# A planned order of two transformers: value matmuls in one set, one PSUM pool, new lag and lead, earlier layer set-up, and a clock in the planner

## Chip, cores and metric

The kernel runs on one core of a Trainium2 chip. The metric is the device time in microseconds of one execution; the median of three runs is compared. Profiles come from one more execution, recorded by the hardware profiler.

## What is computed

The reference is a chain of eight residual stages on `x` of shape 2 x 512 x 128. Stages 4 and 6 are transformers of six layers (`_L2_xcond_ref` and `_L3_xcond_ref`, the same code with other weights), and the change touches only these and the planner that orders their instructions. Each layer has self-attention over 512 tokens, cross-attention to a context of 154 tokens, and a feed-forward part, 16 heads of 8 channels:

```python
for i in range(NL):                       # NL = 6
    xn = _adaln(x, noise_emb, n1_w[i], n1_b[i])
    q, k, v = jnp.split(xn @ qkv_w[i].T, 3, axis=-1)
    a = _attn(_rope(q), _rope(k), v, src_mask).reshape(B, L, D) @ so_w[i].T
    x = x + a
    xn = _adaln(x, noise_emb, n2_w[i], n2_b[i])
    q = _rope((xn @ cq_w[i].T).reshape(B, L, H, HD))
    k = _rope((context @ ck_w[i].T).reshape(B, LC, H, HD))
    v = (context @ cv_w[i].T).reshape(B, LC, H, HD)
    a = _attn(q, k, v, ctx_mask).reshape(B, L, D) @ co_w[i].T
    x = x + a
    xn = _adaln(x, noise_emb, n3_w[i], n3_b[i])
    h = jax.nn.gelu(xn @ f1_w[i].T + f1_b[i], approximate=False)
    x = x + (h @ f2_w[i].T + f2_b[i])
```

(The reshapes of the self-attention are cut.) `_attn` is a softmax over scaled scores, times the values; all is f32.

## The kernel before

A layer is four blocks in the order self-attention of batch 0, of batch 1, cross-attention of batch 0, of batch 1 (`blocks`). A block has four groups of four heads (`Group`). A group passes through two streams.

*Maxima.* For each 128 queries and each head a matmul scores all keys with queries on the partitions (`maximum`: 29 rows of the array, output 512 columns, in a self block; two tiles of 154 in a cross block), and VectorE takes the negated maximum along the keys into `mx`. After the last one, `close` transposes `mx` into `mxT` and four DMAs on SP's queue write it into a spare row of `qT`. A self group has 16 such steps, a cross group 8.

*Exponents.* For each chunk of keys (four chunks of 128 in a self block, two of 77 in a cross block) and each head a matmul scores with keys on the partitions (`exp`: 32 rows, the row with the maxima included, so that the score comes out with its maximum taken off), and ScalarE writes exp of it to a tile `p`. After a chunk's four heads, four value matmuls (128 rows of the array by 32 columns, one for each head, side by side) add the chunk to `av`. `finish` transposes `av` on VectorE and divides by the sum of the exponents. An exponent step of a group is again one head: 16 in a self group, 8 in a cross group.

The driver (the last `with nc.stretch()`) takes one step of each stream in turn; exponents start `LAG` = 24 steps after maxima, and each step adds `STEP` = 0.9 to the turn. When a block's exponents end, `after` projects, adds the residual and, in a cross block, does the feed-forward part, which the next layer's self block of that batch needs; `before` normalises and projects queries, keys and values ahead of a block's first maximum, and its results reach `qT` and `kT` by DMA. `before`, `after`, `close` and `finish` are marked as due `LEAD` = 22 turns earlier. A `Layer` object loads the layer's weights into one of two buffers `lw`, and makes the scale and shift `gb` with twelve small matmul instructions; it is made when the layer's first block is.

Nothing of this sets the order directly. Inside `stretch` all instructions are collected, and `Plan.order` simulates the five queues with estimated durations: it repeatedly takes, over all engines, the ready instruction with the earliest start plus `URGENCY` = 40 ns for each turn. Instructions under `together` are one set and stay adjacent. The plan knows tile buffers (an instruction can't start before all its tiles have a free buffer, and a score matmul also claims the SBUF tile that its evacuation will write), the four by four cells of the TensorE array, and 100 ns for a change of the array's shape. The order is made once for both transformers and issued as planned; `flush` (L344) issues everything, so nearly all rows of the profile carry that line.

PSUM has two pools in these stages: `ms` with seven banks for all scores and projections, and `av` with one. Tiles `p` come from a pool of 16.

In the profile every f32 matmul shows as two instructions: 96 self groups x 4 chunks x 4 heads are 1536 value matmuls, and their row says x3072.

## Time and profile before

| what | value |
|---|---|
| median of three runs (lowest, highest) | 3848.19 us (3847.7, 3848.45) |
| profiled execution | 3844.95 us, span 3843.2 us |
| mean granted TensorE clock | 0.896 |
| first maxima matmul of the first transformer, of the second | 803.2 us, 2322.3 us |
| last exponent (ScalarE, tile p) of the second transformer | 3656.5 us |

Row `p<-ms` of the page's costliest groups is ScalarE's exponents (1211.7 us busy, 606 ns each), `mx<-ms` VectorE's maxima (1297.1 us, 610 ns each), `ms<-kT,qT` and `ms<-kcT,qT` are the maxima's scores, `ms<-qT,kT` and `ms<-qT,kcT` the exponents' scores, and `av<-p,vp` and `av<-p,vcp` the value matmuls. Names ending in c belong to cross blocks. In a timeline, bracketed times are an engine's idle time before a piece and what ended it.

### The profile page before, as it was taken

How to read it: one execution, taken by the hardware profiler on the slowest of the kernel's cores; microseconds unless marked ns; L12 is line 12 of the kernel's file. 1: busy time of each engine (PE TensorE's matmuls, PEld its weight loads, DVE VectorE, ACT ScalarE, POOL GpSimd, SP SyncE). 2: the span in 40 equal slices, each digit the busy share in tenths (PEclk: the TensorE clock that was granted, in tenths of full speed). 3: DMA queues.
4: the chain of work that ended last, by engine and by line, in shares of the span. 5: the costliest groups of instructions: out<-in, count | busy, mean ns of one | idle time of the engine just before them, and what ended most of it. 6: DMA issues, size and time to landing. Idle time of an engine off the chain costs nothing.

```text
span 3843.2 us, 57110 instructions
## 1 busy us (share of the span) xinstructions
PE 3455.9 (90%) x21539; PEld 1931.9 (50%) x21539; DVE 2459.2 (64%) x5712; ACT 1758.4 (46%) x3268; POOL 563.6 (15%) x516
## 2 busy tenths in 40 slices
PE   5598999889999999999999739999999999999937
PEld 3333555455555545555555315555555555555526
DVE  5514555377586766867767477667686776768632
ACT  1122545335455454555545314545455454555550
POOL 2213767310100100010010010010100101010000
PEclk8698999979799988989989768989899998989968
DMA  1000000100000100000000100000000100000002
GB/s 38 1 28 22 1 1 1 38 12 5 10 22 8 28 7 23 10 10 23 8 11 6 42 0 12 8 22 10 11 22 8 28 7 23 10 10 7 8 20 77
DMA packets 179496, 61.01 MB, mean 16 GB/s; under 512 B 169475, under 2 KB 173367, under 8 KB 177559
## 3 DMA queue, kind: packets, MB, share of 16 engines
q1 hardware_dynamic: 177400, 54.72, 6.3%
q8 instruction: 171, 2.80, 0.3%
q10 hardware_dynamic: 1519, 1.74, 0.1%
q14 instruction: 102, 0.84, 0.1%
q0 software_dynamic: 304, 0.92, 0.1%
HBM read 36.37 MB, written 0.52 MB: 10 GB/s over the span
## 4 chain that ended last, share of the span: by engine, by line
PE 67%; DVE 6%; ACT 3%; issue 1%; DMA 1%; POOL 1%; SPq 0%; DVEq 0%; ACTq 0%; POOLq 0%
PE ms L344 50%; PE av L344 14%; PE ms L124 2%; ACT p L344 1%; PE big L124 1%; DVE gate L124 1%; DVE mx L344 1%; DVE avT L344 1%; DVE nrm L344 1%; DMA qT<-rows 1%; ACT L124 0%; DVE ln_st L344 0%; POOL ln_rs L344 0%; DVE aT L344 0%; SPq L344 0%
## 5 line engine op out<-in xcount | busy, mean ns | idle before, releaser
L344 ACT ACTIVATE p<-ms 128x512 f32<-128x512 f32 (+1 forms) x2304 | 1211.7, 606 | 857.5 <-PE ms L344 843.9
L344 DVE TENSOR_REDUCE mx<-ms 128x1 f32<-128x512 f32 (+2 forms) x2316 | 1297.1, 610 | 266.3 <-PE ms L344 256.1
L344 PE MATMUL ms<-qT,kT 32*128 32x512 f32 (+1 forms) x3096 | 933.9, 640 | 3.9 <-ACT p L344 2.4
L344 PE MATMUL ms<-kT,qT 29*128 29x512 f32 x3072 | 916.1, 689 | 13.6 <-DMA qT<-rows 9.0
L344 PEld LDWEIGHTS ms<-qT,kT 32*128 32x128 f32 (+1 forms) x3096 | 382.8, 186 | 231.9 <-ACT p L344 79.5
L344 PEld LDWEIGHTS ms<-kT,qT 29*128 29x128 f32 x3072 | 399.7, 197 | 196.3 <-DVE mx L344 78.9
L344 PE MATMUL ms<-kcT,qT 29*128 29x154 f32 x3072 | 397.3, 347 | 2.8 <-ACT p L344 1.5
L344 PEld LDWEIGHTS ms<-kcT,qT 29*128 29x128 f32 x3072 | 352.8, 209 | 62.7 <-ACT p L344 36.8
L344 POOL TENSOR_TENSOR ln_rs<-ln_ve,mhalf 128x4 f32<-128x4 f32 x96 | 97.7, 1021 | 1899.5 <-DVE ln_ve L344 1899.4
L344 PE MATMUL ms<-qT,kcT 32*77 32x512 f32 x1536 | 352.4, 710 | 9.3 <-DVE mx L344 9.1
L344 PE MATMUL av<-p,vp 128*32 128x512 f32 x3072 | 351.6, 595 | 0.0
L344 DVE STREAM_TRANSPOSE avT<-av 128x512 f32<-128x512 f32 x192 | 137.3, 715 | 237.5 <-PE av L344 235.7
L344 POOL TENSOR_SCALAR p<-p,s 128x666 f32<-128x666 f32 x128 | 249.3, 1960 | 106.7 <-DVE s L344 106.6
L344 PE MATMUL av<-p,vcp 77*32 77x512 f32 x1536 | 229.2, 671 | 2.8 <-DVE avT L344 2.6
L344 PEld LDWEIGHTS av<-p,vp 128*32 128x32 f32 x3072 | 89.3, 109 | 214.5 <-issue 212.2
L344 PEld LDWEIGHTS ms<-qT,kcT 32*77 32x77 f32 x1536 | 117.2, 163 | 124.2 <-issue 67.0
L344 ACT ACTIVATE nrm_t<-ms,gb 128x512 f32<-128x512 f32 x72 | 56.3, 782 | 255.9 <-PE ms L344 238.1
L344 POOL TENSOR_TENSOR turned<-rope_a,rope_s 128x256 f32<-128x256 f32 x144 | 101.3, 728 | 453.6 <-DVE rope_s L344 453.6
L344 DVE TENSOR_TENSOR Y<-Y,ms 128x512 f32<-128x512 f32 x72 | 49.5, 687 | 171.8 <-PE ms L344 171.8
L344 ACT ACTIVATE p<-big,m 128x666 f32<-128x666 f32 x128 | 103.7, 814 | 116.1 <-DVE m L344 115.9
L344 DVE TENSOR_REDUCE m<-big 128x1 f32<-128x666 f32 x128 | 104.1, 846 | 81.7 <-PE big L344 81.7
L344 PE MATMUL ms<-ident,nrm 128*128 128x128 f32 x344 | 76.5, 351 | 74.6 <-DVE nrm L344 71.6
(336 smaller groups left out, 3563.4 us busy)
## 6 DMA issues: line engine op xcount, KB each, us to landing
lw<-in_layers SPq DMA_DIRECT2D x12, 1413.0 KB
ew<-in_w SPq DMA_DIRECT2D x24, 512.0 KB
qT<-rows SPq DMA_DIRECT2D x192, 64.0 KB
qT<-mxT SPq DMA_DIRECT2D x768, 2.0 KB
kT<-rows SPq DMA_DIRECT2D x96, 64.0 KB
wkv<-in_wkv SPq DMA_DIRECT2D x1, 1024.0 KB
f2b<-in_f2b SPq DMA_DIRECT2D x12, 64.0 KB
rv<-in_rows POOLq DMA_DIRECT2D x1, 640.0 KB, 7.3
```

Of the source, the lines that this page charges most:

```text
L124: return getattr(getattr(self._plan.real, self._name), method)(*a, **k)
L344: getattr(getattr(self.real, op.lane), op.method)(*op.a, **op.k)
```

## The change

- The value matmuls of all chunks of a group are issued in one `together` set after the group's last exponent, at the current turn instead of 2.5 later; `av` is taken from the pool `ms` at that moment.
- The pools are eight banks of `ms` and none of `av`.
- 22 tiles `p` instead of 16.
- `LEAD` 30 instead of 22, `LAG` 28 instead of 24.
- `Layer(l + 1)` is made ahead of the first cross block of layer l.
- The planner keeps the use of the array in windows of 3413.3 ns; after a window below 0.42, and in the first, it takes a matmul as twice as long.

```diff
-LEAD, LAG, STEP = 22.0, 24, 0.9
+LEAD, LAG, STEP = 30.0, 28, 0.9
...
+    WINDOW, ENOUGH = 3413.3, 0.42
...
+        use, slow = [0.0], [True]
+
+        def pace(s):
+            w = int(s / self.WINDOW)
+            while len(use) <= w:
+                slow.append(use[-1] < self.ENOUGH)
+                use.append(0.0)
+            return 2.0 if slow[w] else 1.0
...
                     s = max(s, last)
+                    pe = op.takes * pace(s)
+                    use[int(s / self.WINDOW)] += op.takes * len(op.cells) / 16.0 / self.WINDOW
                     for c in op.cells:
-                        cells[c] = s + op.takes + (op.fill if s > last + 10.0 else 0.0)
+                        cells[c] = s + pe + (op.fill if s > last + 10.0 else 0.0)
...
-                done = s + op.takes + op.lands
+                done = s + (pe if op.cells else op.takes) + op.lands
...
-        wide, deep = (2, 3, 1), (0, 7, 1)
+        wide, deep = (2, 3, 1), (0, 8, 0)
...
-                self.tc.tile_pool(name="tfp", bufs=16) as many:
+                self.tc.tile_pool(name="tfp", bufs=22) as many:
...
-                    me.av = self.av.tile([P, 512], F32, name="av")
+                    me.ps = []
...
                         if jj[-1] == 3:
-                            nc.at(turn[0] + 2.5)
+                            me.ps.append(p)
+                        if c == nch - 1 and jj[-1] == 3:
+                            me.av = self.bank()
+                            nc.at(turn[0])
                             with nc.together():
-                                for j in range(4):
-                                    at = (4 * me.g + j) * (HD + 1)
-                                    nc.tensor.matmul(me.av[32 * j:32 * j + 32], lhsT=me.block.vp[:rows, c, at:at + 32], rhs=p[j][:rows],
-                                                     start=c == 0, stop=c == nch - 1)
+                                for c1, p1 in enumerate(me.ps):
+                                    for j in range(4):
+                                        at = (4 * me.g + j) * (HD + 1)
+                                        nc.tensor.matmul(me.av[32 * j:32 * j + 32], lhsT=me.block.vp[:rows, c1, at:at + 32], rhs=p1[j][:rows],
+                                                         start=c1 == 0, stop=c1 == nch - 1)
...
             def blocks():
-                layers = {}
-                for l in range(NL):
-                    for own in (True, False):
-                        for b in range(B):
-                            if l not in layers:
-                                layers[l] = Layer(l)
-                            yield Block(layers[l], b, own)
+                layers = [Layer(0)]
+                for x in range(2 * NL):
+                    l, cross = divmod(x, 2)
+                    for b in range(B):
+                        if b == 0 and cross and l + 1 < NL:
+                            layers.append(Layer(l + 1))
+                        yield Block(layers[l], b, not cross)
```

## The prediction

> **What bounds the kernel now.** I read the core's span and clock first, then the page's busy shares and the chain that ended last, then a table of windows over one transformer layer, and last the timelines of TensorE (PE) and ScalarE (ACT) around one group.

> ```profile
> span 3843.2 us, 57110 instructions
> PE 3455.9 (90%) x21539; PEld 1931.9 (50%) x21539; DVE 2459.2 (64%) x5712; ACT 1758.4 (46%) x3268; POOL 563.6 (15%) x516
> ...
> PE ms L344 50%; PE av L344 14%; PE ms L124 2%; ACT p L344 1%; PE big L124 1%; DVE gate L124 1%; DVE mx L344 1%; DVE avT L344 1%; DVE nrm L344 1%; DMA qT<-rows 1%; ACT L124 0%; DVE ln_st L344 0%; POOL ln_rs L344 0%; DVE aT L344 0%; SPq L344 0%
> ```

> PE looks like the bound: 90% busy, and scores (ms) with value products (av) are 64% of the chain. But the score matmuls use 32 rows of the array each, and several can run at once, so busy time overstates the need. The windows show stages (columns: us, then busy time and instruction count of PE, PEld, DVE, ACT, POOL, the granted clock, DMA share, GB/s).

> ```profile
> 803.00:2142.00 1339.00, 1306.58 (x8790) 734.95 (x8794) 945.23 (x2110) 682.83 (x1276) 99.10 (x126) 0.90 0.07 13
> 2322.00:3631.00 1309.00, 1278.03 (x8818) 715.89 (x8820) 947.22 (x2115) 684.39 (x1280) 99.09 (x126) 0.93 0.07 13
> ...
> 1529.00:1645.00 116.00, 115.12 (x851) 63.98 (x846) 93.86 (x193) 67.24 (x130) 7.17 (x10) 1.00 0.06 9
> 1645.00:1684.00 39.00, 37.48 (x288) 23.05 (x284) 24.48 (x66) 19.40 (x37) 2.43 (x3) 0.78 0.06 9
> 1684.00:1720.00 36.00, 35.12 (x263) 18.13 (x256) 19.63 (x59) 22.48 (x43) 6.97 (x9) 1.00 0.04 6
> 1720.00:1757.00 37.00, 34.67 (x137) 20.03 (x136) 24.43 (x50) 9.47 (x14) 2.28 (x2) 0.73 0.19 52
> ```

> The two transformers hold 2648 of 3843 us. A layer is 228 us: 116 of self-attention groups at full clock with VectorE (DVE) 81% busy, then self to cross (39 us, clock 0.78), cross groups (36), and cross to the next layer (37, clock 0.73, ACT busy 9.5). So I see two losses: inside the self groups, and at the two boundaries of a layer.

> Inside a group, PE's timeline and ACT's:

> ```profile
> 1583.15 0.90 PE L344 MATMUL ms<-qT,kT 32*128 32x512 f32 x2
> 1583.58 2.86 PE L344 MATMUL ms<-kT,qT 29*128 29x512 f32 x15
> 1586.37 3.64 PE L344 MATMUL av<-p,vp 128*32 128x512 f32 x32
> 1589.94 1.99 PE L344 MATMUL ms<-qT,kT 32*128 32x512 f32 x14
> ...
> 1591.16 1.08 ACT L344 ACTIVATE p<-ms 128x512 f32<-128x512 f32 x2 [6.30 <-PE ms L344]
> ```

> PE issues a group's last exponent score (qT,kT) at 1583.15, fills the free banks with maxima scores (kT,qT), does all value products in one run (32 instructions, two per matmul, are all four chunks), and only then issues exponent scores again, 6.8 us later. ACT starves 6.3 us. In PE's timeline 86 of the 96 self groups have this one run of 32, with a median of 6.48 us between the last exponent score before it and the first after. The reason is in the code: pool `many` has 16 tiles p, a group needs 4 chunks x 4 heads = 16, so the next group's first exponent has no tile to write until value products have read one. It is a shortage of p, not of PE.

> [...] 8 value instructions took 1.07 us and 16 took 1.92, so a run costs 2 x 1.07 - 1.92 = 0.22 us beyond its work. [...]

> **The change part by part.** Base: the profiled execution, 3845.0 us with 1.8 outside its span; the median of the runs is 3.2 above it.

> *Value products together, 22 tiles p.* Most self groups already have one run, so joining them is not the main point. Runs still split: 10 self groups (16+16) and 41 cross groups (8+8), 51 in all. Each joined pair saves the 0.22 us[...]: 11 to 23 us, taken 15. The six extra tiles matter more: six exponents (0.50 to 0.57 us each on ACT, 5.01 us for 10 and 4.58 for 8 in ACT's timeline), 3.3 us of ACT work, can be scored before the value products and run beside them. Seven consecutive self periods of a layer are 18.5, 16.8, 17.8, 14.9, 15.2, 14.4 and 13.4 us (every 32nd exponent instruction), mean 15.9, so 84 periods in 12 layers. DVE, 81% busy, becomes the limit at 0.81 x 15.9 = 12.9 us, so the most to gain is 3.0 us a period, 252 us. The least is 0: the six exponents run early, the tiles run out again, and ACT idles just as long before the value run. The planner decides, since a value run waits for the array to drain (a score matmul is two passes of 0.43 us) plus 100 ns in its model, while a score can start at once; turns count 40 ns each, so some maxima still go ahead of the value run. I take 1.2 us a period, two fifths of the most: 100 us.

> *One pool of eight banks.* Before, one bank is a group's `av` from close to finish; after, it is held only from the value run to DVE's transpose (3.64 + 0.72 us and a queue of maxima), and is a score bank otherwise. Gain: one more score in flight. Price: the run can find all eight banks full and wait for one evacuation, 0.6 us (8.46 us for 14 maxima); behind it on PE's queue stand the next scores. Over 84 periods between -25 and +50; I take 0, since the gain and the price concern the same bank.

> *Lead 30.* Projections, norms and feed-forward are due 8 turns (320 ns) sooner. At lead 22 the edge is 880 ns, about the price of draining two passes (0.86 + 0.10), so such a matmul may lose to one more score; at 1200 ns it wins. A boundary's path has about six such PE steps. With 22 boundaries inside the transformers, 0 to 4 us each, I take 1.5: 33 us.

> *Lag 28.* Exponents start four steps later. At each transformer's start maxima run alone and at its end exponents alone, four steps of about 0.55 us at each: 4 x 0.55 x 4 = 9 us more. In the steady state the exponents wait for no maximum now (PEld waits 4.2 us in all for mxT), so nothing is gained there.

> *Layer half a layer ahead.* The weights do not come sooner: for layers 2 to 5 their DMA already waits for the buffer that the layer two before leaves (issued at 1518.4 for a first use at 1691.2). What moves is both DMAs' place in SP's queue, which that wait fixes anyway, 12 small PE instructions (1.18 + 0.28 us, now amid the feed-forward of the boundary), one bank and two DVE operations (0.15 + 0.17). They go where PE has other work: 0 to 20 us over ten boundaries, taken 10.

> *Clock in the ordering.* It adds no instruction; it doubles a matmul's length in the plan after a thin window. Clock means of 0.90 and 0.93 are (0.10 x 1339 + 0.07 x 1309) x 2 = 451 us at half speed, so at most half of that, 225 us, hangs on the clock, but the thin windows come from dependencies that an order cannot remove. Cross groups are thin too and run at 1.00, where a plan that doubles them would be wrong. From -40 to +30, taken -10.

> Sum: -15 - 100 + 0 - 33 + 9 - 10 - 10 = -159 us, so 3686 for the profiled execution and about **3690** as a median of runs.

> **The rivals.**

> *DVE becomes the bound.* If ACT works through the whole value run, self periods fall to 12.9 us: -252, and with the other terms (-59) 3848 - 311 = about 3540. For it: six exponents fill 3.3 of 3.64 us. Against: maxima still go ahead of the value run, and DVE would have to be busy almost without a gap.

> *The gap only moves.* Six exponents earlier, the same idle later: 3848 - 59 = about 3790. For it: between two value runs still exactly 16 exponents must pass. Against: the tiles are freed at once by a single run, and the exponents scored ahead are a backlog for ACT during it.

> *Slower: the boundaries grow.* At 1731 to 1746 the feed-forward of the second batch stands ahead of the last three maxima of the next layer's first group, at half clock, and the exponents restart only after those maxima (ACT waits from 1719.6 to 1751, but for the feed-forward's work). The second batch's feed-forward is due at LAG x 0.9 - LEAD = -0.4 turns from that group's first maximum before, -4.8 after: if its second half (3.84 us) also goes ahead, and the four maxima steps that lag takes from the cover of each boundary (about 1 us each) are missed, ten cross-to-self boundaries lose 7.8 us and twelve self-to-cross ones 4: 126 us. With +9 for the ends, the gains of 15, 10 and 10, and nothing from the tiles, 3848 + 100 = about 3950. It decides once the tiles bring less than 100 / 84 = 1.2 us a period. Against: maxima done earlier are not lost work, and DVE has room in the cross windows.

> *No net change*: the same losses against the main gain.

> **How the numbers follow.** Forecast (3620 to 3760) 0.47; DVE bound 0.15; the gap only moves 0.15; slower 0.19; within 0.2%, which is about what a measurement of this kernel can tell from no change, 0.04. So faster 0.77, same 0.04, slower 0.19. The range of 3550 to 3885 takes in the forecast, the moved gap, half of the DVE case and the nearer part of the slower one. The forecast's own range is 3620 to 3760.

> **What would show it.** Right: exponent scores between the end of one group's scores and its value run, ACT idle before the first p after a value run well below 6.3 us, self periods near 14.7, no value runs of 8, DVE above 81% in the self windows. Wrong: periods still at 15.9 with ACT idle in another place (gap moved); clock in the boundary windows below 0.73 and more than 37 us from the last cross exponent to the next layer's steady groups (boundaries grow); cross windows over 36 us at a clock of 1.00 (the clock model misplans). I would be wrong above all if the plan still puts the value run after a full bank of maxima with ACT's backlog already empty.

## The result, and the profile after

The changed kernel takes 3819.56 us (median of 8 runs, 3806.65 to 3829.62), the kernel before 3857.28 us over its 8 runs of the same comparison (3837.4 to 3884.33). The ratio is 0.9892, with a 95% interval of 0.9854 to 0.993. The forecast was 3690 us, 4.1% below the 3848 us then known. The sign was right; the size was off by a factor of nearly four (4.1% against 1.1%).

The head of the page of the changed kernel, and its chain that ended last:

```profile
span 3817.0 us, 56843 instructions
PE 3396.6 (89%) x21539; PEld 1864.8 (49%) x21539; DVE 2449.4 (64%) x5712; ACT 1762.7 (46%) x3268; POOL 563.2 (15%) x516
...
PE ms L356 61%; PE ms L124 5%; DVE mx L356 4%; PE big L124 2%; PE av L356 2%; PE big L356 2%; POOL turned L356 2%; POOL p L356 1%; ACT p L356 1%; DVE ln_st L356 1%; DVE nrm L356 1%; POOL ln_rs L356 1%; DVE avT L356 1%; DVE Y L356 1%; SPq L356 1%
```

The equal counts of instructions show the same work; VectorE, ScalarE and GpSimd are busy as long as before, and TensorE 59 us less (3455.9 before). "PE av" has gone from the chain mostly because the value products now write a tile named `ms`.

Windows of one layer of the changed kernel (columns as before: us, then busy time and count for PE, PEld, DVE, ACT, POOL, granted clock, DMA share, GB/s): six self periods, a period being the time that one group's 16 exponent steps take, and then the whole layer, from its first self exponent to the next layer's:

```profile
1516.50:1611.00 94.50, 93.26 (x674) 49.21 (x676) 77.08 (x155) 53.82 (x103) 7.09 (x10) 1.00 0.10 23
...
1486.90:1710.10 223.20, 213.83 (x1526) 117.13 (x1524) 161.63 (x369) 119.15 (x222) 18.84 (x24) 0.95 0.08 16
```

The same two stretches of the same layer in the kernel before:

```profile
1543.00:1635.50 92.50, 91.62 (x655) 49.86 (x654) 74.47 (x146) 53.48 (x104) 6.15 (x9) 1.00 0.07 10
...
1522.50:1751.00 228.50, 222.89 (x1527) 125.76 (x1525) 162.83 (x369) 119.08 (x224) 18.85 (x24) 0.92 0.08 15
```

So the periods, which were to shrink from 15.9 to 14.7 us, did not shrink: 92.5 us for six of them before, 94.5 after, at full clock both times. What improved is the clock of the rest: 0.95 instead of 0.92 over the layer. Over the ten layers that are not the first of a transformer, the last six periods of a layer went from 15.5 to 15.8 us.

PE's timeline and ACT's around a value run of the changed kernel:

```profile
1566.60 2.53 PE L356 MATMUL ms<-kT,qT 29*128 29x512 f32 x11
1569.06 3.64 PE L356 MATMUL ms<-p,vp 128*32 128x512 f32 x32
1572.63 2.03 PE L356 MATMUL ms<-qT,kT 32*128 32x512 f32 x12
...
1573.79 3.04 ACT L356 ACTIVATE p<-ms 128x512 f32<-128x512 f32 x6 [6.00 <-PE ms L356]
```

The order is that of before: maxima (kT,qT), the value run, then exponents (qT,kT), and ACT idle for 6.00 us (6.30 before). This run is one of the longer stops: ACT's longest idle time at a whole-group run has a median of 4.61 us, 5.45 before. But over the last six periods ACT idles 6.7 us a period, 6.6 before. The stop is shorter, and the idle time is found elsewhere. Counting exponent scores and value products through PE's timeline of both transformers, 72 of the 96 self value runs start with 22 exponents pending, which are all the tiles. Before, the 96 whole-group runs and halves that end a group started with 16, also all. The median time from the last exponent score ahead of a whole-group run to the first one after it went from 6.48 to 5.77 us.

A layer's parts, measured on ACT's exponents (the layer that starts near 1500 us; the first self exponent to the last, the gap to the first cross exponent, the cross exponents, the gap to the next layer's first):

| kernel | self | gap | cross | gap | sum |
|---|---|---|---|---|---|
| before | 119.9 | 4.1 | 73.2 | 31.3 | 228.5 |
| changed | 136.8 | -0.2 | 86.6 | 0.0 | 223.2 |

The gap of 31 us at the boundary is gone, but the exponents on both sides of it are spread over almost as much more time: the feed-forward and the projections now have exponents around them. This layer gains more than most. Over the eight layers that are neither the first nor the last of a transformer, the mean sum is 226.5 us before and 225.7 after.

**Where the 38 us are.** Every run in the comparisons records its mean granted clock, but for the 8 of the kernel before in the first. In 124 later runs the kernel before has a median clock of 0.890 and the changed one 0.898. The product of time and clock, run by run, has a median of 3436 us before and 3433 us after (8 runs); the rest, time times (1 - clock), is 424 and 390 us. By this account 3 us of the gain are in the work and its waits, and 34 in the clock. It is an account and not a cause: a wait for VectorE at half clock is counted as half lost, too. But within the kernel before, whose instructions and order never vary, the 124 runs follow the clock with a slope of -3535 us per unit and a correlation of -0.94, and they span 3827 to 3883 us. By that slope the 0.008 of clock are 28 us, an estimate somewhat below the 34. One execution shows the same. Both transformers have the same order of instructions; in the windows of the kernel before they are 34 us apart:

```profile
803.00:2172.00 1369.00, 1334.92 (x8978) 746.75 (x8982) 958.21 (x2146) 702.48 (x1311) 101.39 (x128) 0.91 0.07 13
2322.00:3657.00 1335.00, 1302.37 (x8974) 726.31 (x8978) 957.81 (x2145) 701.81 (x1311) 101.39 (x128) 0.93 0.07 13
```

DVE, ACT and POOL have equal busy times in both rows; with a third digit of the clock, 1369 x 0.907 and 1335 x 0.934 are 1242 and 1247 us. In the changed kernel the two are alike:

```profile
803.00:2143.00 1340.00, 1288.73 (x8990) 705.06 (x8993) 953.14 (x2146) 705.18 (x1315) 102.29 (x130) 0.92 0.07 13
2292.00:3628.00 1336.00, 1284.92 (x8993) 702.85 (x8996) 953.17 (x2146) 705.07 (x1315) 102.29 (x130) 0.93 0.07 13
```

So in the two profiled executions the gain lies in the first transformer, 1369 to 1340 us, where the clock was low before; the second, at 0.93 both times, takes 1335 and 1336 us.

### The profile page after: what moved, and what is told of

The parts are those of the page before. It is cut to its first block, busy times and chain, and to the rows that moved or that the text cites. A ratio compares the mean times of both kernels' runs of the same rounds, so it can differ in the third digit from the quotient of the medians.

```text
span 3817.0 us, 56843 instructions
## 1 busy us (share of the span) xinstructions
PE 3396.6 (89%) x21539; PEld 1864.8 (49%) x21539; DVE 2449.4 (64%) x5712; ACT 1762.7 (46%) x3268; POOL 563.2 (15%) x516
## 4 chain that ended last, share of the span: by engine, by line
PE 72%; DVE 16%; POOL 4%; ACT 3%; issue 2%; DMA 1%; SPq 1%; DVEq 0%; ACTq 0%; POOLq 0%
PE ms L356 61%; PE ms L124 5%; DVE mx L356 4%; PE big L124 2%; PE av L356 2%; PE big L356 2%; POOL turned L356 2%; POOL p L356 1%; ACT p L356 1%; DVE ln_st L356 1%; DVE nrm L356 1%; POOL ln_rs L356 1%; DVE avT L356 1%; DVE Y L356 1%; SPq L356 1%
## 5 line engine op out<-in xcount | busy, mean ns | idle before, releaser
L356 DVE TENSOR_REDUCE mx<-ms 128x1 f32<-128x512 f32 (+2 forms) x2316 | 1281.7, 609 | 238.5 <-PE ms L356 234.4
L356 PE MATMUL ms<-kT,qT 29*128 29x512 f32 x3072 | 949.9, 678 | 30.3 <-DMA qT<-mxT 12.3
L356 PE MATMUL ms<-qT,kT 32*128 32x512 f32 (+1 forms) x3096 | 919.7, 632 | 3.2 <-DVE mx L356 2.7
L356 DVE STREAM_TRANSPOSE avT<-ms 128x512 f32<-128x512 f32 x192 | 137.5, 716 | 379.8 <-PE ms L356 379.8
L356 PE MATMUL ms<-kcT,qT 29*128 29x154 f32 x3072 | 353.4, 329 | 25.8 <-DVE mx L356 18.6
L356 PE MATMUL ms<-p,vp 128*32 128x512 f32 x3072 | 353.2, 600 | 0.7
L356 PEld LDWEIGHTS ms<-kcT,qT 29*128 29x128 f32 x3072 | 301.6, 196 | 86.2 <-DVE mx L356 36.0
L356 PE MATMUL ms<-p,vcp 77*32 77x512 f32 x1536 | 199.2, 650 | 0.6 <-DVE mx L356 0.5
L356 PEld LDWEIGHTS ms<-p,vp 128*32 128x32 f32 x3072 | 90.9, 110 | 220.7 <-issue 181.7
L356 PEld LDWEIGHTS ms<-qT,kcT 32*77 32x77 f32 x1536 | 120.0, 148 | 94.5 <-ACT p L356 32.6
L356 PE MATMUL ms<-nrm_t,lw 128*128 128x512 f32 x192 | 136.0, 874 | 1.7 <-ACT nrm_t L356 1.7
```

Source lines behind the costliest of these rows:

```text
L356: getattr(getattr(self.real, op.lane), op.method)(*op.a, **op.k)
```

## The experiments

Ratios are to the kernel before, with their 95% intervals.

### Each part alone, on the kernel before

The value part alone (the hunks of `together`, `self.bank()`, `(0, 8, 0)` and `bufs=22`):

> The kernel before with the value part alone: value matmuls of a group in one set, 22 tiles p, one pool of eight banks. Theory A (the profit of the whole change comes from fewer value runs, 184 planned in place of 242[...]): 0.990 to 0.995 of before. Theory B (the profit is shorter half-clock time at the layer boundaries, from lead and lag): 0.998 to 1.003. Both expect that the self-attention periods do not shrink (mean of the later six in a layer within 0.5 us of before's 15.4), since all 22 tiles are taken before a value run starts; the forecast had them 1.2 us shorter.

Measured: 1.0053 (1.0037 to 1.007), clock 0.884. Slower, and outside both ranges. Fewer value runs did not pay (theory A falls). The periods did not shrink, as both theories said, but neither had them grow: the later six have a mean of 17.8 us, and the self part of a layer takes 135 us from the third layer on.

Lag and lead alone (`LEAD, LAG, STEP = 30.0, 28, 0.9`):

> The kernel before with lag 28 and lead 30 alone. Theory B: 0.988 to 0.994, with fewer half-clock microseconds inside the transformers. Theory A: 1.000 to 1.010, since the plan splits value runs more (344 in place of 242)[...].

Measured: 1.009 (1.0063 to 1.0118), clock 0.885. Theory B falls; sign and size are those of A, and the value runs are split as A has it (344 in the trace, 242 before).

The clock in the planner alone (`pace`, `use`, `pe`):

> The kernel before with the clock in the planner alone. Theory C (the clock in the plan is what pays): 0.987 to 0.995. Theories A and B: 1.000 to 1.012, since the plan splits value runs more (358 in place of 242) and half-clock time stays.

Measured: 1.0201 (1.0154 to 1.0249), clock 0.881, above all three ranges. The half-clock account is 468 us, 44 more than before, and the product of time and clock 3464, 28 more. Made on the order before, the plan with the clock in it gets less clock; it also splits value runs (358), and the two costs were not tried apart.

The layer's set-up half a layer ahead alone (`blocks`):

> The kernel before with the layer's set-up half a layer ahead alone. All theories: 0.996 to 1.002; twelve small matmul instructions leave each boundary (1.5 us each, ten boundaries), and nothing else moves.

Measured: 0.9927 (0.9907 to 0.9947), clock 0.898. It is the only part that pays alone, and brings more than all theories said: 28 us by the medians. The product is 3436, that of before; by the account all of it is clock.

Alone, the four parts come to +0.5, +0.9, +2.0 and -0.7%, a sum of +2.7%; together they give -1.1%. They do not add.

### Each part taken out of the changed kernel

```diff
-                            nc.at(turn[0])
+                            nc.at(turn[0] - 15.0)
                             with nc.together():
```

> The changed kernel with one edit: a group's value set is due 15 turns earlier, so that it goes ahead of further scores. In the plan a self group's value run then starts with 17 or 18 scored exponents pending (22 in 72 of 96 runs now) and 1.2 maxima ahead of it (3.3 now). Theory D (the six extra tiles bring nothing because the plan fills them all before it starts the value run): ScalarE works through the run, the later six self periods of a layer fall by 1 us or more from 15.8, and the ratio to before is 0.96 to 0.98. Theory E (VectorE or the score banks hold the periods, whatever the run waits for): periods within 0.4 us of 15.8, ratio 0.985 to 0.995.

Measured: 0.9903 (0.9876 to 0.9929), no different from the changed kernel. All 96 runs now start with 16 to 19 exponents pending and the median gap is 4.69 us, as theory D wanted, and the time times clock is 3372 us, the least of all kernels here. But the clock is 0.883, so that 449 us are lost by it, and the last six periods of a layer have a mean of 16.2 us (15.5 before, 15.8 in the changed kernel; ten layers, the first of each transformer left out). Theory E is right about time and periods. DVE is busy for 76% of those periods, less than the 80% of before, so it isn't VectorE that holds them; the score banks, its other candidate, were not tried. The two periods with next to no other TensorE work fell to 13.6 and 14.1 us, and those that carry a norm, a projection or the first cross maxima take 18.1 to 19.9 (medians). Part of that is clock: these six periods ran at 0.94 on average, where before and the changed kernel have 1.00. It is not all, since the one layer that ran all six at full clock has a mean of 16.2 as well.

Without the clock in the planner:

> The changed kernel without the clock in the planner. The clock alone cost 2.0% on the kernel before, where it let the plan split value runs (358 in place of 242); with value sets it cannot (166 planned runs with and without it). Theory F (the costs of the parts alone are split value runs, which the sets forbid): within 0.4% of the changed kernel, 0.985 to 0.993 of before. Theory C (the clock in the plan pays): above 0.995. A cost of the clock itself, whatever the sets: below 0.98.

Measured: 0.9964 (0.9948 to 0.998). The clock in the plan pays 0.7% here, where it cost 2.0% alone. Theory C holds inside the change; F, which had the clock worth nothing there, falls.

With lag 24 and lead 22:

> The changed kernel with lag 24 and lead 22. Theory F: within 0.4% of the changed kernel, 0.985 to 0.993 of before. Theory B (lead and lag shorten the boundaries once value runs stay whole): above 0.995.

Measured: 0.9933 (0.9908 to 0.9959). It overlaps the changed kernel's interval: lead and lag are worth a few tenths of a per cent here, if anything, which is nearer to theory F than to B.

With the layer's set-up back at its first block:

> The changed kernel with the layer's set-up back at the layer's first block. If the early set-up is worth the same inside the change as alone (0.9927): 0.994 to 1.000 of before. If its worth was an accident of the order before: 0.985 to 0.993.

Measured: 1.0099 (1.0072 to 1.0125), outside both. A part that the forecast had at 10 us carries 2.1%, 77 us by the medians. The view of tile `gb` tells why; the list of who waited for it in this kernel, and then in the changed one (us, times):

```profile
who waited for it (us, times):
  ACT nrm_t L356: 102.0, 10
```

```profile
who waited for it (us, times):
  PEld ms L356: 26.5, 33
  ACT nrm_t L356: 17.7, 2
```

Two of the ten waits, 17.7 us, stand at the starts of the transformers and are there with the early set-up as well. The other eight, 84 us, are at the ten boundaries between layers: in six of them the norm of the next layer stood ready and ScalarE was idle for 13 to 14 us until `gb` came, in two for 1.8 us. `gb` was due at its turn, and the norm that reads it 30 turns sooner. So the next run gives `gb` the norm's due time at its old place:

```diff
             def __init__(me, l):
-                nc.at(turn[0])
+                nc.at(turn[0] - LEAD)
```

> The changed kernel with the layer's set-up back at the layer's first block, but due LEAD turns earlier like the norm that needs it. Without the early set-up the kernel took 1.0099 of before, and ScalarE waited for gb ten times, 102 us in all (17.7 us in two waits with it). Theory L (that lateness is what the early set-up removes): waits for gb back near 17.7 us, 0.985 to 0.996 of before. Theory M (it is the place of the twelve small matmuls, which leave the array empty in a boundary window, that costs): waits gone, but above 1.000.

Measured: 0.9912 (0.9878 to 0.9945), and the norm's wait for gb is 15.3 us in two waits, those at the starts. Theory L: inside the change the early set-up is worth its due time, not its place.

The same edit on the kernel before:

> The kernel before with the layer's set-up at its old place, due LEAD turns earlier. The early set-up alone gave 0.9927, though no norm waited for gb in the trace before. If its worth there is that the twelve small matmuls leave the boundary's windows: 0.998 to 1.004 here, since they stay in them. If it is the due time: 0.988 to 0.996.

Measured: 1.0263 (1.0231 to 1.0294), outside both. In the kernel before no norm waited for `gb` at a boundary, and the due time does not pay there; but neither expectation has 2.6% more. The clock fell to 0.873, and of the 96 us by the medians the account puts 78 on it. By which of its effects the early set-up pays 0.7% on the kernel before stays open.

### The tiles

> The changed kernel with 16 tiles p. The forecast's main term had the six extra tiles worth 100 us (2.6%). If they only let six exponents run ahead of a value run that starts as late as before (72 of 96 runs start at 22 pending): the ratio stays within 1% of the changed kernel, 0.985 to 1.000 of before. If they are worth the forecast's 100 us: 1.010 to 1.020.

Measured: 1.0098 (1.0068 to 1.0127), just short of the second range. So the tiles are worth 2.1% inside the change, 72 us by the medians, and the last six periods have a mean of 16.5 us without them (at a mean clock of 0.98), 15.8 with them. PE's timeline shows what they mend:

```profile
1567.23 4.92 PE L356 MATMUL ms<-kT,qT 29*128 29x512 f32 x25
1572.09 3.64 PE L356 MATMUL ms<-p,vp 128*32 128x512 f32 x32
```

With sets and 16 tiles, 25 maxima instructions go ahead of the value run here (15 in the run shown of the kernel before); between the last exponent score and a self value run the median is 22, against 13 before and 3 in the changed kernel. All 96 runs start with 16 exponents pending, so no exponent has a tile until the run. That the run itself starts later because the set is no longer open in chunks is argued from the code, not shown. The self part of the layer near 1500 us takes 126 us against 120 before. So the rest of the change lengthens a self period by 1.0 us (15.5 to 16.5), and the six tiles take back 0.7. That the sets are what lengthens it is likely, as sets and tiles together end at +0.5% in the first experiment, but no run has the sets with 16 tiles and nothing else.

### The clock, bought with dummy work

Three matmuls of the whole array in each of the 72 norms, into the bank that the norm's transposes overwrite; they compute nothing that is used. They are to raise the use of the array: in the transformers of the kernel before, of the windows at full clock with less than 0.4 of it in use, 36 of 45 were followed by one at half clock (last section). The 0.86 us of one is an estimate, two instructions at the 0.43 us that successive steps of a value run stand apart:

```diff
-                    ps = self.transposed(self.normed(b, Y))
+                    nrm = self.normed(b, Y)
+                    ps = self.bank()
+                    for _ in range(3):
+                        nc.tensor.matmul(ps, lhsT=Y[:, b * NT, :], rhs=Y[:, b * NT:(b + 1) * NT, :].rearrange("p n d -> p (n d)"), start=True, stop=True)
+                    for i in range(NT):
+                        nc.tensor.transpose(ps[:, i * P:(i + 1) * P], nrm[:, i, :], self.ident)
```

> The kernel before with three dummy matmuls (128 rows, 512 columns, into the bank that the norm's transposes overwrite next) in each of the 72 norms, issued while VectorE and GpSimd make the norm: 216 matmuls of 0.86 us at full clock, 186 us of added TensorE work that computes nothing. Theory K (the granted clock decides the times: before's 48 runs follow it at -3455 us per unit of clock[...]): clock from 0.890 to 0.90 or more, and the time falls or stays, 0.975 to 1.000, in spite of the work. Theory W (work and order decide, the clock only follows): 1.01 to 1.05.

> The changed kernel with the same dummy matmuls. Theory K: clock from 0.898 to 0.91 or more, 0.965 to 0.989 of before. Theory W: 1.00 to 1.04.

> The changed kernel with value sets due 15 turns earlier (0.9903, with a mean clock of 0.883, but a time times clock of 3372 us, 59 less than the changed kernel's 3431), and the same dummy matmuls. Theory K: clock to 0.90 or more, 0.955 to 0.98 of before. Theory W: 1.00 to 1.04.

Measured: on the kernel before 1.0411 (1.0377 to 1.0444), clock 0.898; on the changed one 0.995 (0.9934 to 0.9967), clock 0.922; on the one with earlier value sets 1.0139 (1.0105 to 1.0173), clock 0.909. The clock rose each time, by 0.008, 0.024 and 0.026. In the kernel with earlier value sets the last six self periods, back at a clock of 1.00, fall from 16.2 to 15.1 us, but its first takes 33 us instead of 20. In the changed kernel the account of the clock falls from 390 to 300 us and the product rises from 3433 to 3539: 90 us of clock for 106 of work. On the kernel before hardly any clock is won: the account falls by 13 us only, from 424 to 411. No version gains. Theory K is right that array work can buy clock and wrong that it is worth its price; two of the three came out as theory W said, the third between the two.

### The boundary as a chain

The second batch's feed-forward stands ahead of the next layer's first group, which it does not feed. Here it is due later:

```diff
                     if me.own:
                         return
+                    if b == B - 1:
+                        nc.at(turn[0] + 15.0)
                     xn = layer.adaln(b, 2)
```

> The kernel before with the early layer set-up (0.9927 alone) and one more edit: the second batch's feed-forward is due 15 turns after its step and not LEAD turns ahead, so that the first group of the next layer passes it. Theory P (a layer's time is held by a chain: cross exponents of batch 0, its feed-forward, projections, DMA, the first group's maxima, DMA, exponents; in the kernel before, the other batch's feed-forward stands inside that chain for some 10 us): the stretch from the last cross exponent to the next layer's first self exponent falls from 31 to about 21 us, and the ratio is 0.96 to 0.975. Theory Q (the work is only moved, and the self groups grow by what the stretch loses): 0.985 to 1.000.

> The changed kernel with value sets due 15 turns earlier (0.9903) and the same edit of the feed-forward. Theory P: its stretch of about 29 us falls by some 8 us, 0.955 to 0.975. Theory Q: 0.985 to 1.000.

> The changed kernel with the layer's set-up at the first block but due LEAD turns earlier (0.9912), whose stretch is 29 to 35 us, and the same edit of the feed-forward. Theory P: the stretch falls by some 10 us, 0.955 to 0.975. Theory Q: 0.985 to 1.000.

Measured: 1.0149 (1.0107 to 1.019), 1.012 (1.0094 to 1.0146) and 1.0226 (1.0197 to 1.0255). The gap at the boundary falls, by means over the layers, from 31 to 24 us, from 30 to 24 and from 33 to 28, half or more of what theory P wanted, and the self part grows from 119 to 133, from 126 to 138 and from 120 to 136. ACT's timeline of the first:

```profile
2810.01 3.15 ACT L344 ACTIVATE p<-ms 128x512 f32<-128x512 f32 x6 [23.00 <-PE ms L344]
...
2834.80 0.78 ACT L344 ACTIVATE nrm_t<-ms,gb 128x512 f32<-128x512 f32 x1
2835.60 1.28 ACT L344 ACT_TABLE_LOAD   x1
2836.89 1.51 ACT L344 ACTIVATE hT<-ms,lw 128x512 f32<-128x512 f32 x2
2838.57 0.69 ACT L344 ACTIVATE hT<-ms,lw 128x512 f32<-128x512 f32 x1 [0.17 <-PE ms L344]
2839.43 0.69 ACT L344 ACTIVATE hT<-ms,lw 128x512 f32<-128x512 f32 x1 [0.17 <-PE ms L344]
2847.14 1.28 ACT L344 ACT_TABLE_LOAD   x1 [7.03 <-PE ms L344]
```

The exponents start 23 us after the last cross exponent instead of 31, and are then cut again from 2834.87, when the last one ends, to 2848.44: norm, a load of ACT's table (1.28 us), the feed-forward's `hT`, a second load (1.28 us). Work that filled a gap now stands among work that had none. Theory Q understates it: the ratios are above its range. By the account most of the loss is clock: against the same kernels without this edit, 80 of 81 us in the first, 53 of 82 in the second, 99 of 120 in the third.

## Why the prediction was wrong in size

**The step that failed** is the tile term of *Value products together, 22 tiles p*: "I take 1.2 us a period, two fifths of the most: 100 us". Measured, the last six periods of a layer went from 15.5 to 15.8 us: no gain. The reading of the profile behind it was right in part, since every self value run of the kernel before that ends a group starts with all 16 tiles taken, and the tiles are worth 72 us inside the change (1.0098 without them), 0.7 us a period. Two things were missed. The plan uses up the spare tiles before it starts the value run, 22 pending in 72 of 96, and ACT idles as much per period as before: the rival "the gap only moves". And the rest of the change, the value sets most likely, lengthens a period by 1.0 us, a cost that the sum had at nothing. A third thing goes deeper: the stop at the value run was taken for the loss itself. With value runs that start at 16 to 19 pending it is shorter, and the periods are not. The rival's own time, about 3790 us, is 0.985 of the 3848 then known, just below the measured interval (0.9854 to 0.993).

The bound that I put on that term, VectorE at 12.9 us a period, was no bound that the mean of six periods came near in the runs measured for it (15.1 at the least, in the last of the kernels with dummy work). Even with value runs started at 16 to 19 pending it stayed at 16.2 us, with VectorE at 76%.

**Joining split runs**, -15: the self value runs are all whole, and 44 cross groups have a run of their own while 52 share 26 runs of two groups. The number of runs fell from 242 to 166, more than forecast (42 cross groups were split, not 41, which changes nothing). No gain from it is seen: with 184 runs the value part alone was slower. The 0.22 us a pair make 11 us for 51 pairs; what the term has beyond them was an estimate of mine. In the record of the kernel before, at full clock, a value run starts 0.52 us after the start of the last 512-column score ahead of it (99 of 101 runs), and the next score starts 0.52 us after the start of the run's last instruction (131 of 134), where successive steps of a run stand 0.43 us apart: 0.09 us for a change, near the 100 ns in the plan's model.

**Eight banks**, 0: not tried apart from the sets.

**Lead and lag**, -33 and +9: alone +0.9%, taken out of the change +0.4% with overlapping intervals. Neither figure was shown; alone the sign was wrong.

**Layer ahead**, -10: the price of twelve small instructions was the wrong thing to price. What counts is whether `gb` is ready when the norm is, and with the rest of the change it would not have been: 84 us of waiting at the boundaries, for 77 us of time. The profile before had no such wait, so it could not be read there. The code shows the risk, a norm due LEAD turns ahead of its operand, but LEAD was 22 before and did no harm.

**Clock in the ordering**, -10: it pays 0.7% inside the change (24 us by the medians) and costs 2.0% alone. The size was within its range; but all the other terms were priced as shorter work, while the account finds 34 of the 38 us in the clock. The reason given against the term was misread as well: the window at 1684 that ran at 1.00 is no sample of thin cross groups, since it holds the first batch's feed-forward too, and the stretch at 1645 that was called the way from self to cross is cross exponents and maxima already, at 0.78.

**Slower: the boundaries grow** did not happen in the changed kernel: exponents and maxima of the first self group stand in turn through the second batch's feed-forward. Its mechanism was half right: with that feed-forward out of the way the gap at the boundary does shrink, but three kernels became slower by it.

What remains open is what fixes a self period near 15.5 us when neither ACT (57% busy) nor VectorE (80%) is full and a shorter stop at the value run does not shorten it. PE is busy for 98 to 99% of these periods in its record, but a score takes 32 rows or fewer (forms 32\*128 and 29\*128), and scores overlap: the 14 score instructions after the value run in the prediction took 1.99 us together, where 14 one after another, at the 0.43 us of a value run's steps, would take 6.0. An order free of the planner was not tried.

## What to carry to other kernels

Where a planner makes the order, an edit changes every decision after it: the same small edit was worth -0.7% on one order, -2.1% on another, and a due time alone cost 2.6%; so judge parts inside the whole, by taking them out. A spare buffer may only be filled sooner, so count how many are in use when the instruction that frees them starts (here 22 of 22 in 72 of 96), and ask whether the period, and not only the gap in it, gets shorter. And write a time as time x clock plus time x (1 - clock) before explaining it: where the first part stands still, as here (3436 and 3433 us), look at the record of the clock before shorter work; in these transformers half clock followed 36 of 45 windows with less than 0.4 of the array in use before the change, and 49 of 58 after it. That is an account to start from, not a proof.

## What the runs showed of the hardware

The boundary windows are not idle ones: from 1720 to 1757, at a clock of 0.73, PE is busy for 34.67 of 37 us. The feed-forward at 1731 to 1746, which the prediction has at half clock, ran at half clock up to 1740.3 and at full clock from there. The count does not cover everything: in the other stages of the kernel before only 19 of 44 windows below 0.4 were followed by half clock, and why is open.

The spread of the kernel before (3827 to 3883 us over 124 runs, in one and the same order of instructions) goes with the clock, with the correlation of -0.94 above. It is wider than the three runs known at first let expect, which agreed within 0.8 us, and far wider than the 0.2% that the prediction took for the limit of measurement. Differences under 1% between single executions, or between the profiles of two kernels, say little here: the profiled execution of the kernel with the early layer set-up took 3854 us, the highest of its 19 runs, whose median is 3831.
